# Strip matmuls as one piece in the list that orders a two-layer kernel's engines

## The chip, the cores and the metric

The kernel runs on one core of one Trainium2 chip. The metric is device time in microseconds (us), the median of several executions. Lower is better.

## The reference

Two layers, all in float32. Each layer normalizes x, runs a "mixer" branch s and a "gate" branch g on the normalized rows, and returns x + s * silu(g).

```python
x = L0_attn_x                                  # (4, 1024, 256)
xn = _layernorm(x)
s = _L0_attn_ref(xn, ...)                      # layer 0: linear attention and MLP
g = _silu(_L0_ffn_ref(xn, ...))                # token-shift channel mix
x = x + s * g
xn = _layernorm(x)
s = _L1_attn_ref(xn, ...)                      # layer 1: selective scan (16 states, 512 channels)
g = _silu(_L1_ffn_ref(xn, ...))                # 8 experts, top 2, in sequence
x = x + s * g
...
# the part of layer 0 that the change bears on: Fourier features of q and k, 16 heads of 16
def _fourier_kernel(x, proj_mat):
    p = jnp.einsum('blhd,dm->blhm', x, proj_mat) / math.sqrt(D_HEAD)
    return jnp.concatenate([jnp.cos(p), jnp.sin(p)], axis=-1) / math.sqrt(D_KMAP)
...
qp = _fourier_kernel(q, proj_mat)
kp = _fourier_kernel(k, proj_mat)
kv = jnp.einsum('blhm,blhd->bhmd', kp, v)
attn = jnp.einsum('blhm,bhmd->blhd', qp, kv)
```

## The kernel before

**Work and stages.** The 4096 tokens go in 8 blocks of 512 (TB). Layer 0's attention handles a block in groups: for each of the 4 batches, 8 groups of keys (kind "k", 128 tokens each) and 8 groups of queries (kind "q", 512 tokens by 4 heads). `cycle` runs one group: it projects it to phases, takes the fractions of a turn (`fractions`), the sines and cosines (`sines`), and then uses the features. Between these it steps streams of other work: `before_attention` (q, k, v of the next block), `after_attention` (output projection, MLP, channel mix), and layer 1's scan. The scan has 256 steps (8 blocks, 2 halves of the channels, 16 states); a step costs VectorE a multiply, a scan and a multiply, and adds to y in PSUM by transposing matmuls. Layer 0 runs alone at first; from the first finished block on, scan steps run beside it; when layer 0 is done, the experts (tiles of 256 tokens) run beside the rest of the scan.

**Matmuls on strips.** TensorE's array of 128 x 128 can be used in strips of 32 rows or 32 columns. Five sorts of matmul do so:

- fk (L672, `project_keys`): 32 rows, 8 matmuls a group, two for each of 4 strips, into four PSUM banks.
- fq (L683, `project_queries`): 32 rows, 4 matmuls a group, one for each strip, into four banks.
- kv (L744, `use_keys`): 32 columns, 16 matmuls a group, into two accumulators that are held over a batch.
- pa (L775, `use_queries`): 32 columns, 8 matmuls a group, two for each strip, into one accumulator.
- pt (L847, `prepare_unit`): 16 rows, two matmuls on the same strip, for the scan.

All other matmuls use the whole array. The names in the profile are those of the output tile: tr (transposes, L473), ph and py (MLP; ph, po and pxs in the experts), pi, pz, pd (layer 1's projections), y (L978, scan sums). A float32 matmul counts as two records in the profile, a transpose as one.

**PSUM.** Of the eight banks, two hold y, two the accumulators (tag "acc"), and four are a pool (`bank`, tag "bank", bufs=4) that every other matmul output goes through, in the order of the program. The fractions (ACT L707 or DVE L705, then DVE L708) read fk and fq out of these banks and free them.

**What sets the order.** The program is first written down in one sequence. At the end `arrange` simulates it as a list schedule: every instruction becomes a `_Node` with a weight in ns (`weigh`), it becomes ready when the nodes that it depends on are done, and each engine takes the ready node that is earliest in the program (`heapq` on the index). A node also needs room: each of its tiles' pools must have a free buffer, and it must be that tile's turn in the pool (`room`); a node without room is parked. The order that each of TensorE, VectorE and ScalarE gets this way is then fixed for the chip by dependencies between neighbours. In this simulation a strip matmul occupies its strip for its weight, and the engine for 7 ns only:

```python
start = max([now] + [strips[s] for s in x.strips])
for s in x.strips:
    strips[s] = start + x.weight
free[engine] = start + (7 if len(x.strips) == 1 else x.weight)
```

A whole matmul needs all four strips. On the chip the matmuls run in the order of the list, whatever the simulated times were.

Of the kernel before, what the change touches and what calls it, by code (L numbers as in the profile page):

```python
# [19 lines left out]
PSUM = bass.MemoryType.PSUM  # L20
DRAM = bass.MemoryType.DRAM

P = 128
NB, L, D = 4, 1024, 256
TB = 512
# [36 lines left out]


SIGNAL, LANDING, PER_BYTE = 60.0, 2000.0, 1 / 260
ENGINES = ("PE", "DVE", "Activation")


# [11 lines left out]
class _Node:  # L79


    def __init__(self, i):
        self.i, self.kind, self.engine = i, type(i).__name__, str(i.engine).split(".")[-1]
        self.outs, self.ins = _operands(i.outs), _operands(i.ins)
        self.uses, self.before, self.data, self.after = set(), set(), set(), []
        self.dma = self.kind == "InstDMACopy"
        self.weigh()

    def weigh(self):
        i, kind, engine, outs, ins = self.i, self.kind, self.engine, self.outs, self.ins  # L90
        n = max([_elements(o) for o in outs + ins[:1]] or [0])
        scalars = sum(_elements(o) == 1 for o in ins[1:])
        self.hidden, self.strips, self.bytes = 0.0, (), 0
        if kind == "InstMatmult":
            n = _elements(outs[0])
            self.weight = 0.84 * (max(n, P) if i.is_transpose else 2 * n)
            at, size = i.tile_position or (0, 0), i.tile_size or (P, P)
            self.strips = range(4)
            if size[0] <= 32 or size[1] <= 32:
                self.strips = [at[int(size[0] > 32)] // 32]  # L100
            return
        if self.dma:
            self.weight = 60.0
            if engine == "Pool":
                self.weight = 1300.0 if any(o.dynamic_ap_info is not None for o in outs + ins) else 740.0
            self.bytes = 4
            for _, count in [o for o in outs + ins if o.dynamic_ap_info is None and len(o.ap) > 1][0].ap:
                self.bytes *= count
            return
        w = 40.0  # L110
        if kind == "InstLoadActFuncSet":
            self.weight = 1283.0
            return
        if engine == "Activation":
            w = 165 + 0.84 * n + 75 * min(scalars, 1)
        elif engine == "Pool":
            w = 1250.0 if kind == "InstTensorTensor" else 200 + 0.8 * n
        elif engine == "DVE":
            w = 143 + 1.053 * n
            if kind == "InstTensorScalarPtr":  # L120
                if i.is_tensor_tensor_scan:
                    w = 150 + 2.08 * n + 60 * (scalars > 0)
                elif i.is_scalar_tensor_tensor:
                    w += 60 * (scalars > 0)
                else:
                    psum = any(o.bass_ap.tensor.space == PSUM for o in ins[:1])
                    w = 160 + (1.053 if psum else 0.516) * n + 60 * scalars
            elif kind == "InstTensorCopy":
                w = 160 + 0.6 * n
            elif kind == "InstBNStatsAggregate":  # L130
                w = 170.0
        self.weight, self.hidden = w, 90.0 if w > 190 else 0.0


class _Buffers:


# [4 lines left out]
def arrange(tc, nc, turns, early_pools, late_pools):  # L142

    nodes, names = [], {}
    for i in nc.cur_bb.bb.instructions:
        if type(i).__name__.startswith("BassTile") or type(i).__name__ == "InstRegisterMove":
            continue
        names[i.name] = len(nodes)  # L150
        nodes.append(_Node(i))
    on_chip = (PSUM, bass.MemoryType.SB)
    tensors, tags, tag_of = {}, {}, {}
    early, late = {}, []
    for k, x in enumerate(nodes):
        for writes, ops in ((False, x.ins), (True, x.outs)):
            for o in ops:
                t = o.bass_ap.tensor
                lo, dims = o.bass_ap.offset, o.ap
                if t.space in on_chip:  # L160
                    lo, dims = lo % (o.ap[0][0] or 1 << 40), o.ap[1:]
                hi = lo + sum(s * (c - 1) for s, c in dims) + 1
                if o.dynamic_ap_info is not None:
                    lo, hi = 0, 1 << 40
                tag = getattr(t, "tag", None) if t.space != DRAM else None
                new = t.name not in tensors
                if new:
                    tensors[t.name] = ([], [], set(), [])
                    if tag and getattr(t, "tag_meta", None) is not None:
                        tags.setdefault(tag, _Buffers(t.tag_meta.bufs)).tiles.append(t.name)  # L170
                        tag_of[t.name] = tag
                read, written, users, last = tensors[t.name]
                if tag:
                    pool = tag.rsplit("_", 2)[1]
                    if pool in early_pools:
                        early.setdefault(x.engine, set()).add(k)
                    elif pool in late_pools and new:
                        late.append(k)

                def apart(m, a, b):  # L180
                    return m == k or a >= hi or b <= lo

                whole = lambda a, b: lo <= a and b <= hi
                rows = x.dma and t.space == DRAM
                for a, b, m in written:
                    if not (apart(m, a, b) or (writes and rows and nodes[m].dma)):
                        x.before.add(m)
                        if x.engine not in ("PE", "SP"):
                            x.data.add(m)
                if writes:  # L190
                    if t.space == PSUM:
                        x.before |= set(last)
                        last[:] = [k]
                    x.before |= {m for a, b, m in read if not apart(m, a, b)}
                    read[:] = [r for r in read if not whole(*r[:2])]
                    if not rows:
                        written[:] = [r for r in written if not whole(*r[:2])]
                    written.append((lo, hi, k))
                else:
                    if t.space != DRAM and x.engine != "PE":  # L200
                        same = [r for r in read if nodes[r[2]].engine == x.engine]
                        x.before |= {m for a, b, m in same if not apart(m, a, b)}
                        read[:] = [r for r in read if r not in same or not whole(*r[:2])]
                    read.append((lo, hi, k))
                users.add(k)
                if t.name in tag_of:
                    x.uses.add(t.name)
# [10 lines left out]


    events, ready, order, free = [], {}, {}, {}  # L220
    strips, queue = [0.0] * 4, 0.0
    users = {name: len(tensors[name][2]) for name in tag_of}
    held, touched = set(), set()

# [8 lines left out]

    def room(k):
        new = nodes[k].uses - held
        for name in new:
            of = tags[tag_of[name]]
            if of.free == 0 or of.tiles[of.at] != name:
                of.parked.append(k)
                return False  # L240
        for name in new:
            of = tags[tag_of[name]]
            of.free, of.at = of.free - 1, of.at + 1
            held.add(name)
            again(tag_of[name])
        return True
# [5 lines left out]
    while events:  # L252
        now = events[0][0]
# [15 lines left out]
        while touched:  # L269
            engine = min(touched)  # L270
            touched.discard(engine)
            while ready.get(engine) and free.get(engine, 0.0) <= now:
# [1 line left out]
                if not room(k):  # L274
                    continue
                x = nodes[k]
                order.setdefault(engine, []).append(x.i)
                if x.strips:
                    start = max([now] + [strips[s] for s in x.strips])
                    for s in x.strips:  # L280
                        strips[s] = start + x.weight
                    free[engine] = start + (7 if len(x.strips) == 1 else x.weight)
                    end = start + x.weight + 150
                elif x.dma:
                    free[engine] = now + x.weight
                    queue = max(queue, free[engine] + 300) + x.bytes * PER_BYTE
                    end = queue + LANDING - 300
                else:
                    end = now + x.weight
                    free[engine] = end - x.hidden  # L290
                heapq.heappush(events, (free[engine], k, "free"))
                heapq.heappush(events, (end + SIGNAL, k, "end"))
                for m in x.after:
                    follows = nodes[m].engine == engine and not x.dma and k not in nodes[m].data
                    heapq.heappush(events, (free[engine] if follows else end + SIGNAL, m, "wait"))
    assert sum(len(of) for of in order.values()) == len(nodes)
    for engine in ENGINES:
        for a, b in zip(order[engine], order[engine][1:]):
            tc.add_manual_dep(
# [1283 lines left out]
```

## Time and profile before

| | |
|---|---|
| median of 3 runs | 2305.16 us (2304.19 to 2310.28) |
| profiled execution, its own time | 2302.16 us |
| profiled execution, span first to last instruction | 2300.4 us |
| mean granted TensorE clock | 0.861 |
| TensorE (PE) busy | 1883.4 us, 82% |
| VectorE (DVE) busy | 1941.6 us, 84% |
| ScalarE (ACT) busy | 1395.5 us, 61% |
| GpSimd (POOL) busy | 495.2 us, 22% |
| first / last scan multiply into y's input (DVE L975) | 321.3 / 2270.3 us |
| first / last pa matmul (PE L775) | 115.1 / 1174.5 us |

Busy shares are averages over stages with different limits, so a stage has to be looked at by itself. In the views, a line names the engine, the line of the kernel, the operation, the tiles and the count; a wait is put down to the one that came last. Several lines go through helpers: `accumulate` is L346, `transposed` is L473, `special` (ScalarE functions) is L439.

### The profile page before, as it was taken

The numbers are of one execution on the slowest core, as the hardware profiler recorded it, in microseconds if no ns is written. First come the engines' busy times: TensorE is split into PE (matmuls) and PEld (weight loads), VectorE is DVE, ScalarE is ACT, GpSimd is POOL, SyncE is SP. The second block draws the span as 40 slices with busy tenths as digits, with TensorE's granted clock in tenths as the row PEclk, the third lists the DMA queues.
The fourth block names the chain that finished last, engine by engine and source line by source line (L and its number), as shares of the span: only waits on it lengthen the run. The fifth ranks groups of instructions, "written<-read, shape, count | busy, mean of one in ns | idle before, by whom it ended". The sixth has DMA issues, their size and how long they took to land. (4 is left out here: it accounts for less than half of the span.)

```text
span 2300.4 us, 25432 instructions
## 1 busy us (share of the span) xinstructions
PE 1883.4 (82%) x9192; PEld 1269.7 (55%) x9192; DVE 1941.6 (84%) x2508; ACT 1395.5 (61%) x2039; POOL 495.2 (22%) x459
## 2 busy tenths in 40 slices
PE   6999689779988989989897776378988878898764
PEld 3435356434654544755455554266767577777653
DVE  4563569899988999889899899959979988997998
ACT  4653378777876877787875353335544545454684
POOL 1001100011110011010011020843543324453210
PEclk8789689789988989979898787589999899999866
DMA  9601133423333432323334453677867656767553
GB/s 276 169 0 55 46 84 92 109 66 93 92 83 83 119 80 76 102 66 110 101 93 128 120 179 92 163 208 225 238 190 235 222 191 211 272 216 218 186 173 106
DMA packets 145086, 320.22 MB, mean 139 GB/s; under 512 B 23344, under 2 KB 43952, under 8 KB 139072
## 3 DMA queue, kind: packets, MB, share of 16 engines
q1 hardware_dynamic: 110704, 170.02, 28.1%
q0 software_dynamic: 34256, 148.58, 18.7%
q8 instruction: 73, 1.20, 0.2%
q14 instruction: 53, 0.43, 0.1%
HBM read 256.86 MB, written 61.69 MB: 138 GB/s over the span
## 5 line engine op out<-in xcount | busy, mean ns | idle before, releaser
L439 ACT ACTIVATE da<-dt,neg_a 128x512 f32<-128x512 f32 x512 | 337.2, 716 | 215.2 <-PE y L978 173.4
L978 PE MATMUL y<-ident,da 128*128 128x128 f32 x2048 | 328.1, 308 | 152.6 <-DVE da L975 135.3
L978 PEld LDWEIGHTS y<-ident,da 128*128 128x128 f32 x2048 | 268.4, 158 | 254.4 <-DVE da L975 127.8
L975 DVE TENSOR_TENSOR da<-h,bcs 128x1024 f32<-128x1024 f32 x256 | 312.0, 1219 | 0.6
L957 DVE TENSOR_TENSOR h<-dtu,bcs 128x1024 f32<-128x1024 f32 x240 | 287.7, 1214 | 9.1 <-DMA bcs<-bcd 9.0
L960 DVE TENSOR_TENSOR_SCAN h<-da,h 128x1024 f32<-128x1024 f32 x128 | 291.2, 2284 | 2.1 <-ACT da L439 0.5
L966 DVE TENSOR_TENSOR_SCAN h<-da,h_tail,h 128x512 f32<-128x512 f32 x224 | 278.8, 1273 | 0.6
L346 PE MATMUL ph<-xst,we 128*128 128x256 f32 x736 | 181.3, 402 | 34.9 <-ACT xst L1252 34.6
L346 PEld LDWEIGHTS ph<-xst,we 128*128 128x128 f32 x736 | 144.2, 201 | 60.6 <-ACT xst L1252 39.1
L431 ACT ACT_TABLE_LOAD x134 | 171.9, 1283 | 3.0 <-PEq L1568 0.8
L346 PE MATMUL po<-we,ht 128*128 128x256 f32 x736 | 169.5, 382 | 0.0
L346 PEld LDWEIGHTS po<-we,ht 128*128 128x128 f32 x736 | 137.8, 192 | 23.7 <-issue 4.7
L1264 ACT ACTIVATE ht<-ph,we 128x256 f32<-128x256 f32 x184 | 77.4, 471 | 85.3 <-PE ph L346 82.8
L346 PE MATMUL ph_b<-x3t_b,w_b 128*128 128x512 f32 x256 | 121.6, 618 | 4.0 <-ACT dt L851 2.1
L775 PE MATMUL pa<-fs_q,kvp 128*32 128x512 f32 x512 | 106.3, 702 | 12.5 <-ACT fs_q L439 12.4
L346 PE MATMUL py_b<-w_b,ht_b 128*128 128x256 f32 x512 | 115.7, 381 | 0.3 <-DVE fs_k L708 0.3
L707 ACT ACTIVATE fs_q<-fq,round_c 128x512 f32<-128x512 f32 x112 | 71.2, 688 | 71.0 <-PE fq L683 51.7
L708 DVE SCALAR_TENSOR_TENSOR fs_k<-fs_k,fk 128x512 f32<-128x512 f32 x128 | 81.6, 683 | 32.6 <-ACT fs_k L707 32.3
L346 PEld LDWEIGHTS py_b<-w_b,ht_b 128*128 128x128 f32 x512 | 95.8, 190 | 21.8 <-issue 8.4
L708 DVE SCALAR_TENSOR_TENSOR fs_q<-fs_q,fq 128x512 f32<-128x512 f32 x128 | 82.3, 683 | 24.9 <-ACT fs_q L707 24.3
L744 PE MATMUL kv<-fs_k,v_a 128*32 128x256 f32 x1024 | 83.7, 465 | 23.0 <-ACT fs_k L439 22.9
L683 PE MATMUL fq<-qt_a,bd 32*128 32x512 f32 x256 | 98.9, 709 | 3.8 <-DVE fs_q L708 2.1
(239 smaller groups left out, 3458.1 us busy)
## 6 DMA issues: line engine op xcount, KB each, us to landing
bcs<-bcd SPq DMA_DIRECT2D x240, 512.0 KB, 5.3
xs<-slots POOLq DMA_DIRECT2D x23, 516.0 KB, 4.8
x<-in_x_dram POOLq DMA_DIRECT2D x23, 512.0 KB, 5.0
slots<-blank SPq DMA_DIRECT2D x1, 11776.0 KB, 48.7
w_b<-in_w_dram POOLq DMA_DIRECT2D x16, 512.0 KB, 4.3
w_b<-in_w_dram POOLq DMA_DIRECT2D x32, 256.0 KB, 3.0
xs<-slots POOLq DMA_DIRECT2D x23, 260.0 KB, 5.0
slots<-blank SPq DMA_DIRECT2D x1, 5888.0 KB, 27.2
```

The lines of the kernel that those rows point to most:

```text
L346: nc.tensor.matmul(ps, lhs, rhs, start=i == 0, stop=i == len(pairs) - 1)
L431: nc.scalar.preload_act_table_set({"E": "natural_log_exp_and_others", "S": "silu_and_others"}[which])
L439: in_turn(nc.scalar.activation(out, in_, func, **kw))
L683: nc.tensor.matmul(ps[r], bd_s[rows, par, :], qt[rows, m, :], start=True, stop=True)
L708: nc.vector.scalar_tensor_tensor(t[:, 1, :], t[:, 0, :], -ROUND, ps[r], ALU.add, ALU.subtract)
L744: nc.tensor.matmul(kv[b][r // 2][32 * g : 32 * g + 32, r % 2, :, :], v[:, t, h * DH : (h + 2) * DH], f[:, :, m, par, :], start=(s, t, r % ...
L775: nc.tensor.matmul(pa[b, s][32 * r : 32 * r + 32, :], kvp[b][:, e, 4 * m + r, par, :], features(fs, r)[:, e, :], start=(par, e) == (0, 0), ...
L957: nc.vector.tensor_tensor(h, dtu, bcs[:, 0:1, :].to_broadcast([P, UNIT, TB]), ALU.mult)
L960: nc.vector.tensor_tensor_scan(flat, da.rearrange("p w t -> p (w t)"), flat, 0.0, ALU.mult, ALU.add)
L966: nc.vector.tensor_tensor_scan(h[:, w, :], da[:, w, :], b[w], h_tail[:, c, n : n + 1], ALU.mult, ALU.add,)
L975: nc.vector.tensor_tensor(da, h, bcs[:, 1:2, :].to_broadcast([P, UNIT, TB]), ALU.mult)
L978: nc.tensor.matmul(y[:, t, w * P : (w + 1) * P], da[:, w, t * P : (t + 1) * P], ident, is_transpose=True, start=False, stop=(n, t % 2, w) ...
```

## The change

Only `_Node` and `arrange` change; the instructions that the kernel issues are the same.

- Strip matmuls that follow each other in the program on TensorE, of the same kind (rows or columns) and with the same tiles (inputs for row strips, outputs for column strips), are joined to one node. It is put into TensorE's order as a whole. Its weight is the sum on its fullest strip plus SWITCH (290 ns); the engine is occupied for all of it.
- Every matmul's weight per column goes from 0.84 to COLUMN (0.95).
- `room` gives a node all of its tiles in a pool at once or none.
- Dependencies on PSUM are taken by whole banks.

```diff
+COLUMN, SWITCH = 0.95, 290.0
...
-        self.i, self.kind, self.engine = i, type(i).__name__, str(i.engine).split(".")[-1]
+        self.all, self.i, self.kind, self.engine = [i], i, type(i).__name__, str(i.engine).split(".")[-1]
...
-            self.weight = 0.84 * (max(n, P) if i.is_transpose else 2 * n)
+            self.weight = COLUMN * max(n, P) * (1 if i.is_transpose else 2)
             at, size = i.tile_position or (0, 0), i.tile_size or (P, P)
-            self.strips = range(4)
             if size[0] <= 32 or size[1] <= 32:
-                self.strips = [at[int(size[0] > 32)] // 32]
+                rows = size[0] <= 32
+                of = ins if rows else outs
+                self.strip = (rows, *sorted({o.bass_ap.tensor.name for o in of}))
+                self.load = [0.0] * 4
+                self.load[at[0 if rows else 1] // 32] = self.weight
+                self.weight += SWITCH
...
+    def join(self, other):
+        self.all += other.all
+        self.outs, self.ins = self.outs + other.outs, self.ins + other.ins
+        self.load = [a + b for a, b in zip(self.load, other.load)]
+        self.weight = max(self.load) + SWITCH
...
-        names[i.name] = len(nodes)
-        nodes.append(_Node(i))
+        x = _Node(i)
+        if x.engine == "PE" and x.strip and together and x.strip == together.strip:
+            together.join(x)
+        else:
+            nodes.append(x)
+            if x.engine == "PE":
+                together = x if x.strip else None
+        names[i.name] = len(nodes) - 1
...
+                if t.space == PSUM:
+                    lo, hi = lo // TB * TB, -(-hi // TB) * TB
...
-            if of.free == 0 or of.tiles[of.at] != name:
+            wanted.setdefault(tag_of[name], set()).add(name)
+        for tag, which in wanted.items():
+            of = tags[tag]
+            if of.free < len(which) or set(of.tiles[of.at : of.at + len(which)]) != which:
                 of.parked.append(k)
                 return False
...
-                order.setdefault(engine, []).append(x.i)
-                if x.strips:
-                    start = max([now] + [strips[s] for s in x.strips])
-                    for s in x.strips:
-                        strips[s] = start + x.weight
-                    free[engine] = start + (7 if len(x.strips) == 1 else x.weight)
-                    end = start + x.weight + 150
+                order.setdefault(engine, []).extend(x.all)
+                if engine == "PE":
+                    free[engine] = now + x.weight
+                    end = now + x.weight + 150
```

More of the change, by code (lines that the diff above doesn't have):

```diff
@@ L92, in weigh @@
         scalars = sum(_elements(o) == 1 for o in ins[1:])
-        self.hidden, self.strips, self.bytes = 0.0, (), 0
+        self.hidden, self.strip, self.bytes = 0.0, None, 0
         if kind == "InstMatmult":
             n = _elements(outs[0])
-            self.weight = 0.84 * (max(n, P) if i.is_transpose else 2 * n)
+            self.weight = COLUMN * max(n, P) * (1 if i.is_transpose else 2)
             at, size = i.tile_position or (0, 0), i.tile_size or (P, P)
-            self.strips = range(4)
             if size[0] <= 32 or size[1] <= 32:
-                self.strips = [at[int(size[0] > 32)] // 32]
+                rows = size[0] <= 32
[4 more added lines that the diff above has]
+                self.weight += SWITCH
             return
@@ L142, in arrange @@
 def arrange(tc, nc, turns, early_pools, late_pools):
-    nodes, names = [], {}
+    nodes, names, together = [], {}, None
     for i in nc.cur_bb.bb.instructions:
@@ L220, in arrange @@
     events, ready, order, free = [], {}, {}, {}
-    strips, queue = [0.0] * 4, 0.0
+    queue = 0.0
     users = {name: len(tensors[name][2]) for name in tag_of}
@@ L235, in room @@
         new = nodes[k].uses - held
+        wanted = {}
         for name in new:
-            of = tags[tag_of[name]]
-            if of.free == 0 or of.tiles[of.at] != name:
+            wanted.setdefault(tag_of[name], set()).add(name)
+        for tag, which in wanted.items():
+            of = tags[tag]
+            if of.free < len(which) or set(of.tiles[of.at : of.at + len(which)]) != which:
                 of.parked.append(k)
@@ L295, in arrange @@
                     heapq.heappush(events, (free[engine] if follows else end + SIGNAL, m, "wait"))
-    assert sum(len(of) for of in order.values()) == len(nodes)
+    assert sum(len(of) for of in order.values()) == sum(len(x.all) for x in nodes)
     for engine in ENGINES:
```

## Prediction

> **What bounds the kernel now.** I read the page's busy shares first, then the table by stage, the waits, and last the timeline of TensorE. "Strips" are the matmuls with 32 rows or columns: fk, fq (32 rows), kv, pa (32 columns), pt (16 rows). "Whole" is every other matmul.
>
> The table by stage splits the span at the first scan step (314 us) and where the attention layer's strips end (1200 us). Columns: busy PE, PEld, DVE, ACT, POOL, then the granted clock.
>
> ```profile
> 0.00:314.00 314.00, 254.81 (x1110) 128.89 (x1111) 161.07 (x342) 155.70 (x229) 30.92 (x55) 0.81 0.39 106
> 314.00:1200.00 886.00, 790.73 (x3994) 466.61 (x3993) 800.08 (x1070) 701.69 (x919) 92.66 (x107) 0.90 0.33 91
> 1200.00:2300.00 1100.00, 837.86 (x4091) 674.22 (x4090) 980.49 (x1099) 538.13 (x893) 371.66 (x297) 0.84 0.61 188
> ```
>
> Until 314 us only TensorE is near full (81%); VectorE idles 153 us. From 314 to 1200 TensorE (89%) and VectorE (90%) are both near full, and VectorE idles only 86 us: that is the most this stage can give. After 1200 us VectorE leads (89%) and strips are nearly gone (pt alone).
>
> The timeline of TensorE near 776 us (start, length, a matmul counts as two records, a transpose as one):
>
> ```profile
> 761.87 1.13 PE L683 MATMUL fq<-qt_a,bd 32*128 32x512 f32 x6
> 762.93 0.98 PE L978 MATMUL y<-ident,da 128*128 128x128 f32 x7
> ...
> 776.09 1.05 PE L775 MATMUL pa<-fs_q,kvp 128*32 128x512 f32 x4
> 777.07 0.33 PE L978 MATMUL y<-ident,da 128*128 128x128 f32 x1
> 777.33 1.91 PE L775 MATMUL pa<-fs_q,kvp 128*32 128x512 f32 x12
> 779.17 1.12 PE L683 MATMUL fq<-qt_a,bd 32*128 32x512 f32 x2
> 780.22 0.33 PE L978 MATMUL y<-ident,da 128*128 128x128 f32 x1
> 780.48 1.12 PE L683 MATMUL fq<-qt_a,bd 32*128 32x512 f32 x2
> 781.53 0.55 PE L978 MATMUL y<-ident,da 128*128 128x128 f32 x3
> ```
>
> One fq matmul holds the engine 1.05 us (779.17 to 780.22); three on three strips hold it 1.06 us (761.87 to 762.93). So a group of four in one run costs about 1.07 and in four runs 4.2. The pa group here is torn in two: 0.98 + 1.84 us. Its 12-record run holds both matmuls of some strip, so all 16 would take the same 1.84. Uninterrupted kv and fk groups, and the switch:
>
> ```profile
> 335.46 0.70 PE L346 MATMUL py_b<-w_b,ht_b 128*128 128x256 f32 x2
> 336.09 1.07 PE L744 MATMUL kv<-fs_k,v_a 128*32 128x256 f32 x16
> ...
> 369.10 1.93 PE L744 MATMUL kv<-fs_k,v_a 128*32 128x256 f32 x32
> 370.96 1.15 PE L672 MATMUL fk<-bd,kt_a 32*128 32x256 f32 x16
> 372.04 1.09 PE L978 MATMUL y<-ident,da 128*128 128x128 f32 x8
> ```
>
> kv whole: 1.86 us; fk whole: 1.08. The lone py matmul takes 0.63 where py in a long run takes 0.43: a return to the whole array costs 0.20.
>
> **Part 1, strips in one piece.** Counting runs in the whole timeline: fk 56 runs for 32 groups, fq 66 for 32 (32 of them a single matmul), pa 55 for 32, kv 46, pt 19 for 16. Adding their lengths less idle gaps, and setting beside them the groups at 1.07 (fk), 1.07 (fq), 1.87 (kv), 1.85 (pa), 1.91 (pt, both matmuls on one strip, so no gain):
> - to 314 us: 122 us used; whole groups 56 at full clock, 56/0.81 = 69 at the clock granted; freed 53.
> - 314 to 1200 us: 263 used; 145/0.90 = 161; freed 102.
> - after 1200 us: 17.3 against 17.2; freed 0.
>
> Fewer returns to the whole array: 183 whole runs now, at most 176 pieces after and some 140 if the two kv pieces of a group stay together: (183-140) x 0.20 = 9 us at most; I take 0, since the order is not known.
>
> A piece also waits for the inputs of all its matmuls. The torn pa shows two matmuls going 1.24 us (777.33 - 776.09) ahead; the group's last one waited for its input anyway, so this costs nothing.
>
> How much of this shortens the end? To 314 us, the waits of VectorE put 111 of its 153 idle us down to TensorE rows (py_b 31.8, pv_a 17.1, po_b 12.3, fk 10.6 and smaller). I take 60% of 53: -32 (bounds 0 and -53). From 314 to 1200 the largest waits are:
>
> ```profile
> DVE fs_q L708 <- ACT fs_q L707: 22.2, 24, 2.9
> DVE fs_k L708 <- ACT fs_k L707: 14.7, 13, 3.1
> ...
> ACT fs_q L707 <- PE fq L683: 31.6, 21, 7.0
> ```
>
> VectorE waits for ScalarE's rounding, which waits for fq. First a give-back: a TensorE with gaps is clocked lower. From 500 to 600 us it is 92% busy at clock 0.97; from 400 to 500, 76% at 0.78. If its share falls from 89% to about 79%, these rows put the clock near 0.82, and the 528 us of whole matmuls in the stage grow by 528 x (0.90/0.82 - 1) = 51. Net freed 102 - 51 = 51; half reaches VectorE's idle time: -26 (bounds 0 and -86).
>
> The Trainium skill, "TensorE: Matmul & The Clock Gate", Part 1, has the clock drop to half only after an idle window of about 3.4 us. By that rule gaps shorter than this cost nothing, the net would be 102 and the term an estimated -51; the sum stays with the rows.
>
> **Part 2, four banks at once.** fk and fq write four tiles of a pool of four banks (bufs=4). Now a matmul goes out when its own bank is free; as a piece it waits until the list has all four. A run early on shows the gating by evacuation:
>
> ```profile
> 28.88 2.28 PE L672 MATMUL fk<-bd,kt_a 32*128 32x256 f32 x12 [0.80 <-DVE fs_k L708]
> 31.61 2.04 PE L672 MATMUL fk<-bd,kt_a 32*128 32x256 f32 x4 [0.45 <-DVE fs_k L708]
> ```
>
> The group's last matmul ends as before, but three evacuations that ran meanwhile (0.69 us on ACT L707, then 0.68 on DVE L708) now all follow it: up to 3 x 0.69 = 2.1 us later. Queued behind the piece are all later bank tiles (tr, ph, py, pi, po, pz); free of it are y, kv and pa. 45 groups after 314 us: 95 us at worst; ScalarE is idle 21% there, so some 20 finds nothing to do, and half of that lies where VectorE has a scan step queued: +10. 19 groups before: evacuation is split between ACT and DVE (half, 1.05 us), ScalarE idle half the time: 19 x 1.05 x 0.5 = +10. Bounds 0 and 64 x 2.1 = +134.
>
> The Trainium skill, "TensorEngine Tiling (Array Packing)", Performance Considerations, speaks against the change: tiling speeds up the matmuls but not the evacuation of PSUM, which can become the limit. If all of part 1 were lost to that and the waits of part 2 stayed, the sum would be an estimated +20; the rows above show both effects, and I keep both.
>
> **Part 3, weights, bank-wide dependencies, order.** COLUMN 0.95 for 0.84 and SWITCH 290 add no instruction; they move the simulated times. A 512-wide whole matmul takes 0.86 us at full clock (pc_b, four in 3.44), 0.95 at 0.90, so the new list places TensorE nearer to the trace. Rounding PSUM spans to banks lets the list release the two ReLUs of ph only after both halves (about 0.43 us). No instruction, DMA or queue on SP or POOL is added. After 1200 us only this part acts: no row prices a reordering; VectorE's 120 idle us there bound the gain, and I take 0, with 20 either way (a sixth of that idle time).
>
> **Sum.** -32 - 26 + 10 + 10 + 0 = -38. The profiled execution took 2302.2 us (span 2300.4), 3.0 below the median; 2305.2 - 38 = 2267.
>
> **Rivals.**
> - Full recovery (0.12): VectorE's waits for late fq and fk vanish, the clock holds: -53 - 60 = -113, 2192. For: the page's gate and PE at 95% (41.85 of 44 us) between 106 and 150 us. Against: VectorE at 90% in the long stage.
> - No change (0.09): VectorE sets the pace, TensorE's freed time turns into waits, 2298 to 2312. For: 800 of 886 us busy. Against: the first stage, which has no scan work.
> - Slower (0.27): the four-bank wait. If half of the 134 us is exposed, +67, and part 1 gives only the first stage's -32: +35, 2340. It decides once over (32+26)/134 = 43% of the delay is exposed. For: 32 lone fq matmuls show that banks come free one at a time. Against: y, kv and pa need no bank and fill in.
> - The change doesn't do what it says: not possible in TensorE's order, since a piece is put into the list at one stroke; counted in "no change".
>
> **Numbers.** Forecast as summed 0.52, its own range 2222 (the -26 at -51 and order -20) to 2297 (30% of the 134 exposed, order +10); full recovery 0.12; no change 0.09; slower 0.27. The range 2200 to 2340 leaves out the far ends of the outer two. 0.3% (7 us) is about what a measurement of this kernel can tell from no change: faster 0.52 + 0.12 = 0.64, same 0.09, slower 0.27.
>
> **What would show it.** Right: fq and fk runs in the timeline of 8 and 16 records, 32 each or fewer; strip time near 240 us instead of 402; first scan step near 290 us; VectorE idle after that 15 to 25 us less; clock from 314 to 1200 down to 0.8 to 0.88. Wrong: TensorE waiting before fq or fk for DVE fs rows by more than 1 us a group, ACT L707 waiting more in total than now, or a first scan step after 314 us.

## The result and the profile after

The changed kernel took 2313.5 us (median of 20 runs) against 2303.3 us before (20 runs): 1.005 times, 95% interval 1.0034 to 1.0065. It is slower by about 11 us where 38 us less was forecast; 2313.5 lies inside the stated range, on the other side of zero. Below, 0.001 of a ratio is 2.3 us.

The page's first lines and the table by stage of the changed kernel (columns as before):

```profile
span 2312.7 us, 25432 instructions
...
PE 1827.1 (79%) x9192; PEld 1262.2 (55%) x9192; DVE 1938.6 (84%) x2508; ACT 1391.2 (60%) x2039; POOL 510.3 (22%) x459
```

```profile
0.00:314.00 314.00, 234.90 (x1122) 123.19 (x1123) 163.05 (x344) 156.84 (x231) 31.41 (x57) 0.82 0.39 106
314.00:1200.00 886.00, 744.75 (x3985) 455.02 (x3984) 798.65 (x1071) 698.27 (x916) 85.71 (x105) 0.88 0.32 90
1200.00:2310.00 1110.00, 847.47 (x4089) 683.97 (x4087) 976.92 (x1095) 536.11 (x894) 393.17 (x297) 0.84 0.60 186
```

TensorE has 56 us less to do and VectorE does the same work. But VectorE's busy time from 314 to 1200 us is 799 us as it was: the freed TensorE time bought no work of VectorE in this stage. The first scan multiply (L979) starts at 310.6 us instead of 314.6.

The pieces are there. TensorE's timeline shows them, with what they wait for in brackets:

```profile
26.56 1.98 PE L694 MATMUL fk<-bd,kt_a 32*128 32x256 f32 x16
30.23 3.81 PE L694 MATMUL fk<-bd,kt_a 32*128 32x256 f32 x16 [1.70 <-DVE fs_k L730]
...
124.13 1.15 PE L705 MATMUL fq<-qt_a,bd 32*128 32x512 f32 x8
126.15 2.95 PE L797 MATMUL pa<-fs_q,kvp 128*32 128x512 f32 x16 [0.86 <-ACT fs_q L461]
129.03 2.37 PE L705 MATMUL fq<-qt_a,bd 32*128 32x512 f32 x8
133.44 5.01 PE L797 MATMUL pa<-fs_q,kvp 128*32 128x512 f32 x16 [2.05 <-ACT fs_q L461]
```

Every fk run has 16 records or a multiple, every fq run 8 or 16, every pa run 16. Counting the whole timeline, 140 runs on strips take 328 us; before, 242 runs took 402. The second fk group now waits 1.70 us for its banks and starts at 30.23 instead of 28.88. A piece does not take its full-clock time either (pa 2.95 and 5.01 us, not 1.85): it waits inside for the inputs of its matmuls (2.95 us at a granted clock of 1.00), and some run at a lower clock (0.66 granted over the 5.01 us).

Where the time went shows in VectorE's waits over the whole span. Columns: us in total, times, longest. First the kernel before, then the changed one:

```profile
DVE es L1277 <- PE po L346: 71.6, 18, 24.6
DVE fs_k L708 <- ACT fs_k L707: 32.3, 16, 14.1
DVE fs_q L708 <- ACT fs_q L707: 24.3, 28, 2.9
DVE h L960 <- ACT da L439: 0.5, 1, 0.5
```

```profile
DVE h L982 <- ACT da L461: 41.8, 14, 11.6
DVE h L988 <- ACT da L461: 33.2, 12, 5.7
DVE dt L879 <- ACT ln L461: 28.4, 4, 14.9
DVE es L1299 <- PE po L368: 18.9, 10, 5.4
DVE fs_k L730 <- ACT fs_k L729: 12.9, 9, 2.8
DVE fs_q L730 <- ACT fs_q L729: 9.8, 7, 4.9
```

The scan on VectorE (h) now waits 75 us for its decays (da, an exponential on ScalarE), which it practically never did. Summed over all rows, VectorE's waits for TensorE fell from 231 to 158 us and for ScalarE's rounding (fs) from 57 to 23; h on da rose from 0.5 to 75, dt on ln from 9 to 28, and the rest from 51 to 80. In all 348 became 364 us. Span less this sum is 1952 us before and 1948 after: **VectorE's idle time is the difference between the two kernels, and the gain was turned into a new wait.** By stage these waits went from 151 to 149 us before 314 us, from 84 to 86 until 1200 us (fs 26 us less, h on da 24 more), and from 113 to 129 after it: the loss lies after 1200 us. ScalarE's side of it is in the page's groups, before and after (last column: idle time before the decays, and for what):

```profile
L439 ACT ACTIVATE da<-dt,neg_a 128x512 f32<-128x512 f32 x512 | 337.2, 716 | 215.2 <-PE y L978 173.4
```

```profile
L461 ACT ACTIVATE da<-dt,neg_a 128x512 f32<-128x512 f32 x512 | 335.6, 715 | 171.7 <-PE y L1000 98.3
```

A decay needs a free da buffer, which y's transposes give back. Before, ScalarE stood at the decays early and waited for y; now it waits less there. But the decays did not move back in its order. The same scan step shows what did move; its decays on ScalarE and its scan on VectorE, before and after:

```profile
1564.95 1.34 ACT L439 ACTIVATE da<-dt,neg_a 128x512 f32<-128x512 f32 x2
1577.97 2.28 DVE L960 TENSOR_TENSOR_SCAN h<-da,h 128x1024 f32<-128x1024 f32 x1
```

```profile
1568.72 3.78 ACT L461 ACTIVATE da<-dt,neg_a 128x512 f32<-128x512 f32 x6
1570.08 2.29 DVE L982 TENSOR_TENSOR_SCAN h<-da,h 128x1024 f32<-128x1024 f32 x1 [7.41 <-ACT da L461]
```

The decays (the first two of the six) come 3.8 us later, but VectorE had come to its scan 15 us earlier (at 1562.7). Counted over the traces, 174 of the 256 scan steps now have fewer other instructions ahead of them in VectorE's order and 12 have more (4.6 fewer on average); of the decays in ScalarE's order 127 have fewer and one more (2.2 fewer). **VectorE takes the scan steps earlier, further than the decays moved, and catches up with ScalarE.** When a step's last multiply starts (L997), the decays of 1.47 further steps are done on average; before it was 2.17.

Not all of the 75 us is of this kind. The longest wait, 11.6 us at 1510 us, comes where ScalarE itself stands idle for 26.7 us until GpSimd has set the first column of dt (L900). Before, it stood there 20.1 us for the same, and VectorE waited 24.6 us at that place for po.

### The profile page after: what moved, and what is told of

Same layout as the page of the kernel before. It is cut to its first block, busy times and chain, and to the rows that moved or that the text cites. A ratio compares the mean times of both kernels' runs of the same rounds, so it can differ in the third digit from the quotient of the medians.

```text
span 2312.7 us, 25432 instructions
## 1 busy us (share of the span) xinstructions
PE 1827.1 (79%) x9192; PEld 1262.2 (55%) x9192; DVE 1938.6 (84%) x2508; ACT 1391.2 (60%) x2039; POOL 510.3 (22%) x459
## 5 line engine op out<-in xcount | busy, mean ns | idle before, releaser
L1000 PE MATMUL y<-ident,da 128*128 128x128 f32 x2048 | 312.3, 304 | 158.0 <-DVE da L997 150.5
L982 DVE TENSOR_TENSOR_SCAN h<-da,h 128x1024 f32<-128x1024 f32 x128 | 291.5, 2282 | 42.5 <-ACT da L461 41.8
L997 DVE TENSOR_TENSOR da<-h,bcs 128x1024 f32<-128x1024 f32 x256 | 311.2, 1216 | 0.5
L979 DVE TENSOR_TENSOR h<-dtu,bcs 128x1024 f32<-128x1024 f32 x240 | 287.6, 1210 | 20.6 <-DMA bcs<-bcd 20.2
L368 PE MATMUL ph<-xst,we 128*128 128x256 f32 x736 | 192.6, 420 | 39.0 <-ACT xst L1274 35.8
L368 PEld LDWEIGHTS ph<-xst,we 128*128 128x128 f32 x736 | 152.4, 213 | 66.9 <-ACT xst L1274 38.8
L1237 POOL DMA_INDIRECT fused<-xs x46 | 97.4, 2118 | 44.7 <-DVE xs L1303 32.3
L797 PE MATMUL pa<-fs_q,kvp 128*32 128x512 f32 x512 | 87.9, 705 | 11.4 <-ACT fs_q L461 11.4
L1274 ACT COPY xst<-pxs 128x512 f32<-128x512 f32 x46 | 26.9, 584 | 106.1 <-PE pxs L1270 106.0
L1251 POOL DMA_INDIRECT we<-in_wcat_dram,wrow x46 | 73.3, 1594 | 71.7 <-ACT xst L1274 23.0
```

Source lines behind the costliest of these rows:

```text
L368: nc.tensor.matmul(ps, lhs, rhs, start=i == 0, stop=i == len(pairs) - 1)
L797: nc.tensor.matmul(pa[b, s][32 * r : 32 * r + 32, :], kvp[b][:, e, 4 * m + r, par, :], features(fs, r)[:, e, :], start=(par, e) == (0, 0), ...
L979: nc.vector.tensor_tensor(h, dtu, bcs[:, 0:1, :].to_broadcast([P, UNIT, TB]), ALU.mult)
L982: nc.vector.tensor_tensor_scan(flat, da.rearrange("p w t -> p (w t)"), flat, 0.0, ALU.mult, ALU.add)
L997: nc.vector.tensor_tensor(da, h, bcs[:, 1:2, :].to_broadcast([P, UNIT, TB]), ALU.mult)
L1000: nc.tensor.matmul(y[:, t, w * P : (w + 1) * P], da[:, w, t * P : (t + 1) * P], ident, is_transpose=True, start=False, stop=(n, t % 2, w) ...
```

## Experiments

Three theories. **Path**: TensorE's strip time is not what sets the end. **Banks**: the wait for four banks eats the gain. **Weights**: the new simulated times give the other engines a worse order.

**1. Only kv and pa as pieces**

```diff
-if x.engine == "PE" and x.strip and together and x.strip == together.strip:
+if x.engine == "PE" and x.strip and not x.strip[0] and together and x.strip == together.strip:
```

> Only kv and pa are joined to pieces; fk, fq and pt are single nodes again and take one bank at a time (each then holds the engine in the simulation for its own weight plus SWITCH). Against the changed kernel, which is 1.005 of before. Banks theory (four banks at once eat what the pieces free): the wait goes, the pieces of kv and pa keep their gain, so 15 to 30 us faster than the changed kernel, 0.988 to 0.995 of before. Path theory (strip time of TensorE is not on the path that sets layer 0's pace): within 6 us of the changed kernel, 1.002 to 1.008. Weights theory (the new weights and the order they give cost the 10 us): like the path theory.

Measured 1.0058 (1.0036 to 1.008). Taking the four-bank wait away gains nothing; the banks theory fails in this form. Single fk and fq nodes are dearer in the simulation, though, so the two could also cancel.

**2. Only fk, fq and pt as pieces**

```diff
-if x.engine == "PE" and x.strip and together and x.strip == together.strip:
+if x.engine == "PE" and x.strip and x.strip[0] and together and x.strip == together.strip:
```

> Only fk, fq and pt are joined; kv and pa are single nodes. Banks theory: the four-bank wait stays and kv and pa are torn, so slower than the changed kernel by 5 to 15 us, 1.007 to 1.012 of before. Path theory: within 6 us of the changed kernel. If the tearing of kv and pa is what costs TensorE most (they have 1536 of 2304 strip records), slower by more than 15 us.

Measured 1.1082 (1.105 to 1.1114): 238 us slower than the changed kernel, far beyond the 5 to 15 us of the banks theory. The theory of torn kv and pa said only "more than 15 us", and its reason is not there: on the chip kv and pa run together nearly as in the changed kernel (24 of 30 kv runs have 32 records, 27 of 31 pa runs have 16), and strips take 357 us for 328. What differs is the simulation. A single kv node is charged 0.95 x 512 + 290 = 776 ns, 512 of them 397 us, where 64 pieces of 1263 ns were 81; pa goes from 72 to 323 us. The list believed in 567 us of TensorE time that does not exist, and the chip lost 238 us. VectorE's waits in this kernel:

```profile
DVE h L982 <- ACT da L461: 99.6, 27, 10.9
DVE x L619 <- PE py_b L368: 70.1, 14, 14.4
DVE h L988 <- ACT da L461: 54.0, 16, 9.3
```

The same new wait, doubled to 154 us. This run turned the study to the weights.

**3. The old weight of a column**

```diff
-COLUMN, SWITCH = 0.95, 290.0
+COLUMN, SWITCH = 0.84, 290.0
```

> The change with COLUMN back at 0.84; pieces, SWITCH and bank spans as changed. Weights theory: the 6 us lost among the experts and the 5 us lost at the end of layer 0 come from the slower simulated TensorE, so 8 to 12 us faster than the changed kernel, 1.000 to 1.002 of before. Banks and path theories: the pieces alone decide, within 4 us of the changed kernel, 1.003 to 1.007.

Measured 0.9961 (0.9937 to 0.9985): 20 us faster than the changed kernel, more than the weights theory expected. h on da is down to 7.2 us.

**4. PSUM dependencies by address**

```diff
-if t.space == PSUM:
-    lo, hi = lo // TB * TB, -(-hi // TB) * TB
```

> The change without rounding PSUM dependencies to whole banks. If the later release of the first of two ReLUs (ph) in the list costs the experts their 6 us: 4 to 8 us faster than the changed kernel, 1.001 to 1.003 of before. All other theories: within 3 us, 1.004 to 1.006.

Measured 1.0028 (1.0007 to 1.0049). Up to 1200 us the trace agrees with the changed kernel's within about a microsecond; some 10 us come back among the experts in the profiled run, 5 by the ratios, whose intervals overlap.

**5. The kernel before with the new weight alone**

```diff
-self.weight = 0.84 * (max(n, P) if i.is_transpose else 2 * n)
+self.weight = 0.95 * (max(n, P) if i.is_transpose else 2 * n)
```

> The kernel before with one number changed: 0.95 for 0.84 as weight of a column; strips simulated as before, no pieces. Weights theory (a slower simulated TensorE gives an order that is worse on the chip, with or without pieces): 10 to 25 us slower than before, 1.004 to 1.011. If the weight only hurts together with the pieces, which hold the simulated engine: within 6 us of before, 0.997 to 1.003.

Measured 0.988 (0.9847 to 0.9913): 28 us faster, where the weights theory said slower. "A slower simulated TensorE is worse" is wrong as a general rule. Strips are torn here as before (228 runs, 382 us).

**6. Every fk and fq matmul twice, same list** (in the traces TensorE, VectorE and ScalarE keep the changed kernel's orders)

```diff
-for m in range(NC):
+for m in (0, 1, 0, 1):
...
-for r in range(4):
+for r in (0, 1, 2, 3, 0, 1, 2, 3):
...
+if any(o.bass_ap.tensor.name.startswith("bd") for o in ins):
+    self.weight /= 2
```

> The changed kernel with every fk and fq matmul done twice in its piece and half its weight, so that the list is the same and TensorE gets some 64 x 1.07 / 0.88 = 78 us more to do before 1200 us. If TensorE's time sets layer 0's pace at the rates of the prediction (about a half): 30 to 45 us slower than the changed kernel, 1.018 to 1.025 of before. Path theory (it lies beside the evacuations and sines): up to 12 us, at most 1.010.

Measured 1.0023 (1.0001 to 1.0045), not slower than the changed kernel (1.0034 to 1.0065). The fk and fq groups of the profile grew from 128 to 191 us busy, and this cost nothing:

```profile
0.00:314.00 314.00, 240.75 (x1339) 133.76 (x1340) 155.51 (x336) 152.93 (x225) 30.55 (x55) 0.85 0.37 105
314.00:1200.00 886.00, 762.68 (x4530) 476.00 (x4529) 807.10 (x1078) 700.44 (x921) 86.75 (x107) 0.93 0.31 91
```

Part of it was paid by the clock: 0.93 granted from 314 to 1200 us instead of 0.88, so all other matmuls went faster. For this list, and net of the clock, the path theory holds for fk and fq.

**7. VectorE's absolute value twice, nearly the same list**

```diff
 magnitude(t[:, 0, :], t[:, 1, :])
+EXTRA.add(magnitude(t[:, 0, :], t[:, 1, :]).ins.name)    # weight 0 in weigh()
```

> The changed kernel with VectorE's absolute value of the phases (146 instructions, 0.68 us for most, some 90 us in all, before 1200 us) done twice, the second at no weight in the list; it is on the way from fk and fq to kv and pa. If VectorE with ScalarE sets layer 0's pace: 50 to 90 us slower than the changed kernel, 1.027 to 1.045 of before, far more for each us added than twice the matmuls. If TensorE sets it: under 30 us.

Measured 1.0298 (1.0263 to 1.0333): 57 us slower than the changed kernel for 82 us more on VectorE (166 for 84 us in its groups), 0.7 us for each. TensorE's added 63 us cost none. But the second absolute value adds a step to the simulation although its weight is 0, and the list moved: ScalarE's order differs from the changed kernel's at 166 of 2039 places. So a part of the 57 us may be the order's. On the way from fk and fq to kv and pa, VectorE sets layer 0's pace, as far as this run can tell.

**8. Pieces with the old weight and no price for the switch**

```diff
-COLUMN, SWITCH = 0.95, 290.0
+COLUMN, SWITCH = 0.84, 0.0
```

> The change with COLUMN 0.84 and SWITCH 0: pieces cost nothing extra in the simulation. Weights theory: another step to a faster simulated TensorE, 2 to 8 us faster than with COLUMN 0.84 and SWITCH 290 (0.9961 of before), so 0.993 to 0.996. If SWITCH stands for time that the list must leave (a switch is real on the chip): slower, 0.998 to 1.003.

Measured 0.988 (0.9848 to 0.9911), 28 us faster than before, better than expected. VectorE's waits:

```profile
DVE es L1299 <- PE po L368: 68.4, 22, 23.4
...
DVE fs_k L730 <- ACT fs_k L729: 17.6, 13, 3.8
DVE fs_q L730 <- ACT fs_q L729: 10.1, 13, 1.8
DVE h L982 <- ACT da L461: 2.3, 2, 1.7
DVE h L988 <- ACT da L461: 0.6, 1, 0.6
```

The waits for the fractions are halved as in the changed kernel, and the decays are in time as before the change. From here SWITCH 290 costs 19 us (to 0.9961) and COLUMN 0.95 another 20 (to 1.005). In the other order (experiment 9) COLUMN costs 32 us and SWITCH 8: together 39, and the split depends on the path.

**9 to 13. Other values of the weights**

Experiment 9 is the change with SWITCH 0, experiments 10 and 11 are the kernel before with 0.90 and 1.00, experiment 12 is the change with COLUMN 0.90, and experiment 13 has COLUMN 0.75 and SWITCH 0.

> The change with SWITCH 0 and COLUMN 0.95 as changed. If SWITCH is what costs (it made 0.988 to 0.996 at COLUMN 0.84): 0.985 to 0.996 of before. If each order is a draw within about 1% (lottery theory: small moves of the simulated times reshuffle the list, and the sign of a single result says nothing of the edit): anywhere from 0.985 to 1.010, with no sum of the separate effects to be seen. If the two effects add up (0.009 each): 0.996.

> The kernel before with 0.90 for 0.84 (0.95 gave 0.988). Trend theory: in between, 0.992 to 0.996, since a whole matmul's time at the granted clock lies above 0.84. Lottery theory: anywhere from 0.985 to 1.010.

> The kernel before with 1.00 for 0.84. Trend theory: 0.983 to 0.990, at or just past the best. Lottery theory: anywhere from 0.985 to 1.010, so above 0.995 is against a trend.

> The change with COLUMN 0.90 (0.84 gave 0.996, 0.95 gave 1.005). Trend theory: 0.999 to 1.002. Lottery theory: anywhere from 0.985 to 1.010, outside 0.996 to 1.005 as likely as inside.

> Pieces with COLUMN 0.75 and SWITCH 0. Trend theory (with pieces, each step to a faster simulated TensorE was faster: 1.005, 0.9975 and 0.996 with SWITCH 290, 1.002 and 0.988 with 0): 0.975 to 0.985. If there is a best value near what a whole matmul takes on the chip at full clock (0.84): 0.988 to 1.000.

All results on the weights together; the next three columns are sums over VectorE's waits in us, from the one profiled execution of each kernel (up to 9 us from its median). "Lead" is the mean number of further scan steps whose decays are done, counted in the trace as above:

| list | column | SWITCH | ratio (95%) | h on da | es on po | all | lead |
|---|---|---|---|---|---|---|---|
| before | 0.84 | | 1 | 0.5 | 71.6 | 348 | 2.17 |
| before | 0.90 | | 0.9936 (0.9906 to 0.9966) | 22.2 | 41.8 | 327 | 1.92 |
| before | 0.95 | | 0.988 (0.9847 to 0.9913) | 31.2 | 14.3 | 316 | 1.65 |
| before | 1.00 | | 1.0045 (1.0029 to 1.0061) | 57.1 | 10.0 | 357 | 1.45 |
| pieces | 0.75 | 0 | 1.0127 (1.0096 to 1.0157) | 0.7 | 82.8 | 377 | 2.35 |
| pieces | 0.84 | 0 | 0.988 (0.9848 to 0.9911) | 2.9 | 68.4 | 320 | 2.04 |
| pieces | 0.84 | 290 | 0.9961 (0.9937 to 0.9985) | 7.2 | 69.2 | 336 | 1.93 |
| pieces | 0.90 | 290 | 0.9975 (0.9952 to 0.9997) | 46.9 | 36.6 | 332 | 1.57 |
| pieces | 0.95 | 0 | 1.0017 (1.0 to 1.0034) | 73.3 | 20.0 | 353 | 1.53 |
| pieces | 0.95 | 290 | 1.005 (1.0034 to 1.0065) | 75.0 | 18.9 | 364 | 1.47 |

With strips at 7 ns, and with pieces at SWITCH 0, the time falls and rises again: a valley, as far as four and three points show one. That the lead and both waits move in order with the weight speaks against a mere draw. In both families the wait of the scan for its decays grows with the column's weight, as the lead shrinks, and the experts' wait for TensorE (es on po) shrinks too. The low end has more to it: from 0.84 to 0.75 these two waits explain 12 of 57 us; VectorE's other waits for TensorE grew by 20. The best value is near 0.95 where strips hold the simulated engine for 7 ns, and near 0.84 (of those tried) where a piece holds it throughout. The change moved both at once and went past the bottom. The trend theory of experiment 13 (lower is always faster) fell.

**14. kv and pa gathered after the simulation.** The kernel before with its own list; only TensorE's order is regrouped, each group of kv and of pa at the place of its last matmul. Doing the same with fk and fq was not tried: a matmul moved past work that depends on its evacuation can block.

```diff
+    for i in order["PE"]:
+        of = group.get(i.name)        # the kv or pa matmuls of i's group
+        if of is None:
+            pe.append(i)
+            continue
+        left[id(of)] = left.get(id(of), len(of)) - 1
+        if left[id(of)] == 0:
+            pe.extend(of)
+    order["PE"] = pe
```

> The kernel before with its own list for every engine, except that in TensorE's order the kv and the pa matmuls of a group are moved together to the place of the group's last one (fk and fq stay torn). So strips are whole without any change of the simulated times. If untorn strips are worth what the prediction took: pa falls from 102.6 us to about 75 and kv by some us, half of it reaches the end, 10 to 20 us faster, 0.991 to 0.996 of before. Path theory: within 6 us, 0.997 to 1.003.

Measured 0.9937 (0.9913 to 0.9962), 14 us faster: pa fell from 103 to 89 us, and layer 0's last gate comes 13.6 us earlier. On this list untorn strips pay.

**15. The same on the list with weight 0.95**

> The same on the list of the kernel before with 0.95 as weight (0.988 of before). Path theory: within 6 us of that, 0.986 to 0.991. If untorn strips pay: 0.979 to 0.984, and this is the best version.

Measured 0.9885 (0.9849 to 0.992) where the list without regrouping has 0.988: nothing. So what untorn strips are worth depends on the list; a part of the 14 us may be the order's.

**16. Experiment 8 with dependencies by address**

> Pieces with COLUMN 0.84, SWITCH 0 (0.988) and PSUM dependencies by address instead of by bank. Without spans the changed kernel went from 1.005 to 1.003 and lost its 6 us among the experts. If that carries over: 0.984 to 0.987. If each order is a draw: 0.983 to 0.995.

Measured 0.9923 (0.9899 to 0.9947), against 0.988 with spans: the other sign than in experiment 4. The intervals overlap both times: bank spans are worth a few us at most, and their sign is not shown.

**17 and 18. COLUMN split in two**

```diff
# 17: transposes at 0.84, the rest at 0.95
+self.weight = 0.84 * max(n, P) if i.is_transpose else COLUMN * max(n, P) * 2
# 18: transposes at 0.95, the rest at 0.84
+self.weight = COLUMN * max(n, P) if i.is_transpose else 0.84 * max(n, P) * 2
```

> The change with 0.84 for transposes alone (the scan's y, 2048 of them, gives its da buffer back); all other matmuls keep 0.95 and SWITCH 290. Over the whole span VectorE's scans wait 75 us for ScalarE's decays (h on da) in the changed kernel, 0.5 before, 7 with COLUMN 0.84. Theory of the turns (y late in the simulation, so decays late in ScalarE's order): this wait falls under 20 us and the time to 0.990 to 0.998 of before. Theory of all matmuls (everything later on TensorE moves the decays back): it stays at 45 to 75 us and the time at 1.000 to 1.006.

> The converse: 0.95 for transposes, 0.84 for all other matmuls, SWITCH 290. Theory of the turns: the wait of h on da at 40 us or more, 1.000 to 1.006 of before. Theory of all matmuls: under 20 us, as with COLUMN 0.84 throughout, 0.994 to 0.999.

Experiment 17: 1.0011 (0.999 to 1.0032); experiment 18: 0.9938 (0.9912 to 0.9963). The rows that decide, of 17 and then of 18:

```profile
DVE h L982 <- ACT da L461: 35.7, 15, 9.0
DVE h L988 <- ACT da L461: 27.3, 13, 4.8
```

```profile
DVE h L988 <- ACT da L461: 7.2, 6, 2.3
DVE h L982 <- ACT da L461: 6.4, 4, 2.3
```

63 us against 13.6. The new wait comes with the weight of all the other matmuls, not with that of the transposes.

The best versions, experiments 5, 8 and 15, agree at 0.988 and beat both kernels. They reach it with torn strips, with pieces, and with half of the strips gathered.

## Why the prediction was wrong, by its steps

- **Part 3 is the step that failed.** It put the weights at 0, "with 20 either way". From pieces at the old weight without SWITCH (0.988) to the change as made (1.005) they cost 39 us (19 for SWITCH and 20 for COLUMN, or 32 for COLUMN and 8 for SWITCH, by the order in which they are set), of the 49 between forecast and result. What they do is move scan steps ahead in VectorE's order, until the scan waits for its decays (0.5 us before, 75 after). The step argued that 0.95 lies nearer to a whole matmul's time on the chip; with the pieces a truer time did not make a better list. Nothing in the profile before showed the wait that it opened (h on da, 0.5 us), so 20 was no bound for it.
- **Part 1, the size.** Torn strips were read rightly, and the pieces form as the diff says. But 74 us were freed, not 155: 122 to 103 us in the first stage (19, not 53) and 263 to 207 in the second (56, not 102), because pieces wait inside and some run at the lower clock, as torn strips had (pa records over 900 ns: 111 of 512, before 110). What each of the two took was not separated. Strips at 240 us were forecast; 328 were measured.
- **Part 1, the share that reaches the end.** 60% and a half were taken. The first scan step came 4 us earlier, not 24, and VectorE's idle time from 314 to 1200 us stayed (86, now 87). Doubling fk and fq at no cost shows that their time has no such share in the changed list. In the list of before 14 us less pa came with 14 us less in all (experiment 14), and in the list with 0.95 with nothing (experiment 15): there is no fixed share. That experiment 8 comes near the forecast (28 us faster, forecast 38) does not save the reason: experiment 5 gets the same 28 with strips torn.
- **The clock.** The rows put it at 0.82 for a TensorE that is 79% busy. As less was freed, it was 84% busy, at 0.88, which is what the same two rows give for 84%; the whole matmuls of the stage grew from 528 to 538 us, 10 and not 51 (12 by 0.90/0.88). So the term was too large because the freed time was. By the rule of the Trainium skill, "TensorE: Matmul & The Clock Gate", Part 1, as the prediction cites it, short gaps would have cost nothing; the row at 133.44 speaks against that, with a clock of 1.00 until 131.4, 2.05 us of idle time and then 0.66. Nor does the busy share alone set the clock: it was 0.90 at 89% before and 0.93 at 86% in experiment 6.
- **Part 2.** The waits of fk for banks appear (1.70 us in the row above), but they are few: TensorE waited 12.3 us for the fractions (fs) before fk and fq in all 64 groups, 5.3 before the change. Leaving fk and fq apart gained nothing (experiment 1). None of the prediction's three signs of being wrong came: ScalarE's waits at the fractions fell, and the first scan step was not late. The 20 us were not confirmed; since the list changed with it, their true size stays open.
- **The slower rival.** The sign was given 0.27, with the four banks as mechanism. The sign came, by another mechanism.
- **The rival "no change".** It had 0.09, and its mechanism came nearest: VectorE sets the pace, and TensorE's freed time turns into waits (348 to 364 us). The result is 1.5 us above its 2298 to 2312.
- **What held.** VectorE's idle time is the right measure: in the kernels of the table span less that sum is 1948 to 1957 us. It has to be summed over the whole span, with room for waits that do not exist yet.

Open: why VectorE's scan steps move further ahead than ScalarE's decays when TensorE is simulated slower. That work which needs TensorE becomes ready later in the simulation, so that the list takes scan steps in its place, fits the code and the orders, but no run here shows the simulated times.

## What to carry to other kernels

Where a simulated list orders in-order engines, a weight is a control over all of them: changing TensorE's weight by an eighth moved the end by 20 to 32 us with no instruction changed. A wait that a model's weight removes on one engine can come back as another where that engine overtakes the one that feeds it. Sweep the weights after any change to the model before judging the change itself. To learn whether an engine's time matters, add some to it with the list unchanged (and see in the trace that it is), and do the same on its rival; here 63 us on TensorE cost nothing and 82 us on VectorE, with the list a little moved, cost 57.

## What was not expected of the hardware

More work made TensorE's clock faster: with fk and fq doubled, the granted clock from 314 to 1200 us rose from 0.88 to 0.93, and TensorE's busy time rose by 26 us (1827.1 to 1853.0) for 63 us more of fk and fq. A pa record takes 592 ns at its shortest and 1063 at its longest, and pieces that follow a wait often run at the longer value: 70 of the 128 records of pieces that TensorE waited before take over 900 ns, 41 of the 384 others. In the row at 133.44, after a wait of 2.05 us, most records take 1.06 us at a granted clock of 0.66.
